# Offset rows and edge biases of a two-layer graph network: where they are added, and when shared one-hots are turned

## The chip, the core and the metric

The kernel is one program on one core of a Trainium2 chip. The metric is the device time of an execution in microseconds (us). The kernel before has a median of 10060.64 us over three runs (10058.67 to 10062.71). One further execution was recorded with the hardware profiler. It took 10882.62 us, and the durations in this document come from it.

## The reference, cut to what matters

A graph of 10,000 nodes (rows of 512 fp32 values) and 160,000 edges, sorted by `dst`, with eight attributes an edge, goes through two layers.

```python
# layer 0: a gated mixture of 4 experts, the top 2 of each node, each expert two SAGE convolutions
aggr = segment_sum(h[src], dst) * inv_deg
h = relu(aggr @ W_l + b_l + h @ W_r)              # twice for each expert
x = layernorm(x + sum(sel * top_v))
# layer 1: attention over the edges, 8 heads of 64, and a feed-forward net
z = layernorm(x)
q = (z @ Wq.T + bq).reshape(n, 8, 64)             # k and v in the same way
s = einsum('ehd,ehd->eh', q[src], k[dst]) / 8 + edge_attr_8
p = exp(s - segment_max(s, src)[src])
alpha = p / segment_sum(p, src)[src]
att = segment_sum(alpha[:, :, None] * v[dst], src) @ Wo.T + bo
x1 = x + att
ff = silu(layernorm(x1) @ W1.T + b1) @ W2.T + b2
out = layernorm(x + x1 + ff)
```

Two kinds of addends matter here. The *offsets* are rows of 512 that are the same for every node: `b_l` of each expert's second convolution, `bq`, `bk`, `bv`, `bo`, `b2`. The *edges' biases* are the eight values of `edge_attr_8` that are added to an edge's eight scores before the softmax.

## The kernel before, in words

Nodes are worked on in 79 blocks of 128 (`NB`). A block has four windows of 32 nodes (`NQ`, `W`), and a window has up to five chunks of 128 edges (`CAP`). Edges are brought to their nodes by gathers of whole rows (indirect DMAs that GpSimd issues) and by products of TensorE with one-hot matrices. There are three stages.

**First stage** (0 to about 3976 us of the trace). The first convolution of all experts (L1187) and the products of its result with the second convolution's neighbour weights (L1197), which go to memory as `y_tab`; the hidden rows themselves go to `h_tab`. They take the nodes' sums by one-hot products (L1148) of gathered rows; the one-hots are made on VectorE (L899, used by both stages). Beside this the edges are sorted for the attention (L1057). PE, VectorE, ScalarE and GpSimd run here in the order in which the program is written (`manual_schedule`). Near the end, in the third block group from the last, nine offset vectors go through `split_rows` (L715 to L730). A bf16 value holds fewer digits than an fp32 one, so the function cuts each offset into three rows of bf16 whose sum is the offset. It takes ten VectorE instructions on a tile of three partitions, eleven where a second vector is added first (`fold_s`, what the normalization's own offset contributes to queries, keys and values), and a load and a store on the SP queue. The rows are kept in memory as `rows_s`. From 3976 to about 4258 us the stage runs out.

**Second stage** (4258 to about 7720 us): the second convolution, its weighted sum over experts, two normalizations, and queries, keys and values. Only PE and GpSimd keep the written order; the scheduler places the work of VectorE, ScalarE and the SP queue. `bias_rows` (L732) loads seven offsets' three rows into a tile of 128 partitions that is zero elsewhere, and makes a tile of ones (`onesb`); a matmul of the two adds an offset to all rows of a product that stands in PSUM. In each block TensorE does, in this order:

1. Rounds 0 to 2 (L1417): one-hot products of the gathered `y` rows, accumulated in two PSUM tiles `p_ag`, 24 matmuls. Behind each round GpSimd issues four gathers (L1323) into buffers of a ring of 12.
2. Of the block before, the transposes of `z` (L1331), copied by ScalarE to `z_t`.
3. `own(b, 0)` and `own(b, 1)`: for an expert, a load of `hb` (L1375, six buffers, SP queue), four matmuls (L1378), the offset's matmul (L1379), and two VectorE products of the PSUM tile with the gate factors in `pick` (L1382 or L1385), which build the sums `t[0]` and `t[1]`. `own` of a block adds to tiles that `p_ag` joins at the block's end.
4. `fetch(b + 2)`: one-hots (L899) and gather addresses `ix` for the block after next.
5. Rounds 3 and 4 of L1417, the two-round burst.
6. `own(b, 2)` and `own(b, 3)`.
7. Of the block before, keys, values and queries: four matmuls each (L1340) and the offset's matmul (L1342). ScalarE copies keys (L1344) and values (L1346) into `kvt`, which goes to `kv_all` in memory; the query is scaled and cut into three bf16 parts by ScalarE and VectorE in turn (L1354 to L1359).
8. VectorE and ScalarE join `p_ag` and `t` (L1439), rectify (L1441), add to `x` (L1442) and normalize twice, to `x1` and `z`.

A row of `kv_all` has 1032 words (`KVW`): 512 of keys, and for each head 64 values and a one. The one makes the weighted sum yield the softmax's denominator as a 65th column.

**Third stage, the attention** (7720 to about 10880 us). A loop over windows (L1805), four steps `j` = 0 to 3 a block, with PE, VectorE, ScalarE and GpSimd in written order. A window's edges that sort to its own nodes fill four chunks; a fifth, shared by the block's four windows (`kvo`), takes the overflow. A step holds several windows at once, each at another point of its path:

- gathers of the rows of `kv_all` two steps ahead (L1543, through `pull` and `pull_over`);
- `expand` (L1780): one-hot products that bring the queries to the edges, in PSUM (`qe`); `expand_over` does it for the shared chunk;
- `score` (L1817): VectorE multiplies the keys by `qe`, in place, in two halves of two chunks; the reduction L1853 sums 64 products a head, and L1856 adds the edges' biases, which lie in `meta`. For the shared chunk `score_over` (L1794 to L1798) does the three things once a block, at j=3, and L1811 copies its scores to each window's `s`;
- `weigh`: a maximum over chunks into `wide` (L1682), its transpose on TensorE (L1684, "the row"), a maximum (L1687), a spread by matmul (L1689), subtraction (L1691), exponential (L1694, ScalarE), the product of one-hots and exponentials (L1703, three chunks on GpSimd, two on VectorE), weighted sums (L1717), denominators (L1722, L1723), scaling (L1726), a transpose (L1728);
- `turned` (L1565 to L1570): transposes of bf16 one-hots on TensorE and a copy by ScalarE; `turn_hots` for a window two steps ahead, and `over_t`, the four shared chunks of the next block, at the end of step j=2 (L1849). The PSUM tile `turns` holds the transposed `wide`, the spread maximum and these transposes;
- `open_block` (from L1510), behind j=1: one-hots of the block after next by comparison (L1518) and a copy (L1524).

Between these fixed places a small planner, `advance` (L1742), runs *jobs*: `front` (output weights, first residual, normalization, transposes), `back` (feed-forward, L1625 and L1635 with the Silu L1627 between them) for two blocks at once, `tail`. A job is a generator. It yields the cost of its next piece, and `advance(rate)` lets pieces run as long as credit lasts; a piece that yields 0 runs at most once at each call, so each `yield 0` puts what follows one call later. In `front` two of them stand between the offset's matmul (L1587) and `x2` (L1591), which VectorE adds; L1598, on GpSimd, adds the residual once more.

## Time and profile before

| | us |
|---|---|
| median of three runs | 10060.64 |
| the profiled execution | 10882.62 |
| its span, first to last instruction | 10880.8 |
| TensorE busy | 9845.5 |
| weight loads busy (beside TensorE) | 5639.8 |
| GpSimd busy | 6889.5 |
| VectorE busy | 5280.1 |
| ScalarE busy | 3011.4 |
| stretch of the first stage and its end | 0 to 4258 |
| stretch of the second stage | 4258 to 7720 |
| stretch of the attention | 7720 to 10880 |

The profiled execution is the longer one, by 8%; its mean granted clock of TensorE is 0.967. A group of the profile is one line with one engine and one form of operands: after the name and the shapes stand the count, behind the first bar the busy time in us and the mean duration of one instruction in ns, behind the second bar the idle time of the engine just ahead of these instructions, with what ended it. "issue" there is idle time for which the trace shows no wait. PE is TensorE, PEld its weight loads, DVE VectorE, ACT ScalarE, POOL GpSimd, SP the queue engine. GpSimd counts the time of its gathers' issue as busy (L1323 in the second stage, L1543 in the attention). The times of instructions are counted from the span's start.

### The profile page before, as it was taken

How to read it: one execution, taken by the hardware profiler on the slowest of the kernel's cores; microseconds unless marked ns; L12 is line 12 of the kernel's file. 1: busy time of each engine (PE TensorE's matmuls, PEld its weight loads, DVE VectorE, ACT ScalarE, POOL GpSimd, SP SyncE). 2: the span in 40 equal slices, each digit the busy share in tenths (PEclk: the TensorE clock that was granted, in tenths of full speed). 3: DMA queues.
4: the chain of work that ended last, by engine and by line, in shares of the span. 5: the costliest groups of instructions: out<-in, count | busy, mean ns of one | idle time of the engine just before them, and what ended most of it. 6: DMA issues, size and time to landing. Idle time of an engine off the chain costs nothing.

```text
span 10880.8 us, 168764 instructions
## 1 busy us (share of the span) xinstructions
PE 9845.5 (90%) x63574; PEld 5639.8 (52%) x63887; DVE 5280.1 (49%) x8244; ACT 3011.4 (28%) x5827; POOL 6889.5 (63%) x6736
## 2 busy tenths in 40 slices
PE   7999999999999988899998989899788888888888
PEld 4666666666666654333333333333455555555555
DVE  7888960000000021333333333333588888888886
ACT  1111111111111111111111111111266666666665
POOL 5566666666666664666666666666566666666664
PEclk9999999999999999999999999999799999999999
DMA  6544544444444434777777777777577777777774
GB/s 208 175 155 159 159 151 148 139 147 139 148 151 144 152 121 162 250 258 253 252 262 249 251 251 262 251 252 255 193 247 248 248 246 246 242 250 242 248 246 133
DMA packets 1076313, 2256.12 MB, mean 207 GB/s; under 512 B 250459, under 2 KB 500214, under 8 KB 1074720
## 3 DMA queue, kind: packets, MB, share of 16 engines
q0 software_dynamic: 588224, 1654.56, 47.8%
q1 hardware_dynamic: 479546, 576.99, 15.8%
q10 hardware_dynamic: 7718, 13.65, 0.4%
q8 instruction: 508, 8.32, 0.3%
q14 instruction: 317, 2.60, 0.1%
HBM read 2174.00 MB, written 378.96 MB: 235 GB/s over the span
## 4 chain that ended last, share of the span: by engine, by line
PE 78%; issue 8%; DVE 8%; ACT 4%; another core or an unknown queue 2%; DMA 1%; POOL 0%; ACTq 0%; SPq 0%; DVEq 0%; POOLq 0%
PE mm L1187 19%; PE mm L1378 10%; PE mm L1197 10%; PE mm L1340 8%; PE p_ag L1417 7%; PE p_ag L1148 4%; PE bank L1625 4%; PE bank L1635 4%; PE sums L1717 3%; DVE m L927 2%; PE bank L1585 2%; PE qe L1780 2%; DVE s L1853 2%; ACT L1627 1%
## 5 line engine op out<-in xcount | busy, mean ns | idle before, releaser
L1123 POOL DMA_INDIRECT ring<-in_x_dram,idx_t x1580 | 1929.2, 1221 | 1234.9 <-PE p_ag L1148 688.7
L1187 PE MATMUL mm<-tt,big 128*128 128x256 f32 (+1 forms) x8960 | 1980.9, 379 | 24.0 <-issue 23.4
L1187 PEld LDWEIGHTS mm<-tt,big 128*128 128x128 f32 x8960 | 1686.3, 191 | 324.8 <-issue 92.7
L1057 POOL DMA_INDIRECT sorted<-pay,addr x1250 | 1265.6, 1012 | 380.4 <-issue 356.5
L1378 PE MATMUL mm<-big,hb 128*128 128x512 f32 x2528 | 1241.9, 623 | 144.2 <-issue 127.8
L1323 POOL DMA_INDIRECT y<-y_tab,ix x920 | 932.8, 1014 | 479.7 <-issue 226.8
L1197 PE MATMUL mm<-wn,h 128*128 128x512 f32 x2528 | 1133.2, 598 | 18.6 <-issue 16.8
L1543 POOL DMA_INDIRECT kv<-kv_all,meta x948 | 974.0, 1027 | 260.1 <-issue 203.2
L1323 POOL DMA_INDIRECT ring<-y_tab,ix x660 | 686.5, 1040 | 558.5 <-PE p_ag L1417 272.5
L1189 ACT ACTIVATE h<-mm,bl 128x256 f32<-128x256 f32 (+1 forms) x640 | 294.8, 470 | 2527.3 <-PE mm L1187 1366.0
L1340 PE MATMUL mm<-big,z_t 128*128 128x512 f32 x1896 | 908.2, 619 | 60.6 <-DVE t L1385 28.9
L899 DVE TENSOR_TENSOR oh<-loc_t,iota_w 128x640 f32<-128x640 bf16 x158 | 129.9, 823 | 1687.7 <-remote 853.2
L1703 POOL TENSOR_TENSOR ohp<-oh,p 128x768 f32<-128x768 bf16 x316 | 466.1, 1475 | 695.5 <-ACT p L1694 694.9
L1378 PEld LDWEIGHTS mm<-big,hb 128*128 128x128 f32 x2528 | 486.1, 198 | 787.0 <-issue 741.3
L1197 PEld LDWEIGHTS mm<-wn,h 128*128 128x128 f32 x2528 | 468.3, 190 | 630.9 <-issue 617.3
L1441 ACT ACTIVATE t<-t,gsel 128x512 f32<-128x512 f32 x158 | 109.2, 722 | 2285.6 <-DVE t L1439 1644.9
L1625 PE MATMUL bank<-big,big 128*128 128x256 f32 (+1 forms) x2560 | 626.0, 388 | 91.8 <-ACT big L1627 66.7
L1417 PE MATMUL p_ag<-y,oh 128*32 128x512 f32 x3680 | 592.2, 600 | 76.6 <-issue 66.0
L1340 PEld LDWEIGHTS mm<-big,z_t 128*128 128x128 f32 x1896 | 371.1, 198 | 546.0 <-issue 481.6
L1635 PE MATMUL bank<-big,big 128*128 128x512 f32 x1264 | 592.3, 599 | 3.2 <-ACT big L1609 0.7
L1817 DVE TENSOR_TENSOR kv<-qe,kv 128x1024 f32<-128x1024 f32 x474 | 575.1, 1213 | 28.5 <-DMA kv<-kv_all,meta 28.4
L1625 PEld LDWEIGHTS bank<-big,big 128*128 128x128 f32 x2560 | 477.2, 195 | 210.0 <-ACT big L1627 103.7
(298 smaller groups left out, 14314.6 us busy)
## 6 DMA issues: line engine op xcount, KB each, us to landing
y_tab<-y SPq DMA_DIRECT2D x632, 256.0 KB
hb<-h_tab SPq DMA_DIRECT2D x316, 256.0 KB
h_tab<-h SPq DMA_DIRECT2D x156, 512.0 KB
kv_all<-kvt SPq DMA_DIRECT2D x79, 516.0 KB
xb<-in_x_dram SPq DMA_DIRECT2D x156, 256.0 KB
q_all<-q SPq DMA_DIRECT2D x79, 384.0 KB
q<-q_all SPq DMA_DIRECT2D x237, 128.0 KB
ring<-in_x_dram,idx_t POOLq DMA_INDIRECT x1580
```

The lines of the kernel that those rows point to most:

```text
L1057: inst = nc.gpsimd.indirect_dma_start(out=sorted1[:], out_offset=bass.IndirectOffsetOnAxis(ap=addr_i[:, c0 + c:c0 + c + 1], axis=0), in_=p ...
L1123: nc.gpsimd.indirect_dma_start(out=gbuf[i % GB], out_offset=None, in_=x, in_offset=bass.IndirectOffsetOnAxis(ap=window(idx_t, b)[:, j, c:c ...
L1187: nc.tensor.matmul(ph[:, :n], w[:, k, f * P:(f + 1) * P], tt[:, i, k, :n], start=(i + k == 0), stop=(i == 1 and k == KD - 1))
L1197: nc.tensor.matmul(py, h[:, k, i * P:(i + 1) * P], wn[e][:, k, :], start=(k == 0), stop=(k == KD - 1))
L1323: nc.gpsimd.indirect_dma_start(out=ybuf[i % YB], out_offset=None, in_=y_flat, in_offset=bass.IndirectOffsetOnAxis(ap=ahead[b][1][:, j, c:c ...
L1340: nc.tensor.matmul(po, z_t[:, k, :], wqkv[i][:, k, :], start=(k == 0), stop=False)
L1378: nc.tensor.matmul(pr, hb[:, k, :], wr[e][:, k, :], start=(k == 0), stop=False)
L1417: nc.tensor.matmul(p_ag[v][j * W:(j + 1) * W, :], oh[:, j * CAP + c, :], g[:, v * D:(v + 1) * D], start=(c == 0), stop=(c == CAP - 1))
L1543: nc.gpsimd.indirect_dma_start(out=to, out_offset=None, in_=kv_all[:], in_offset=bass.IndirectOffsetOnAxis(ap=blocks[b][0].bitcast(I32)[:, ...
L1625: nc.tensor.matmul(ph, up(f, k), z_t[:, k, :m], start=(k == 0), stop=(k == KD - 1))
L1635: nc.tensor.matmul(po, hid[:, k, i * P:(i + 1) * P], w2[k // KD][:, k % KD, :], start=(k == 0), stop=False)
L1817: nc.vector.tensor_tensor(k, qe.pop((w, g)), k, op=ALU.mult)
```

## The change

In the second stage the seven offset matmuls (L1379, L1342) go. The offsets come as rows of 512 fp32 on all 128 partitions, by seven broadcast loads on ScalarE's DMA queue at the stage's start, and VectorE adds them as it reads the product from PSUM. In `own` the sum goes to a new tile `mine`, from which the two products with `pick` then read. Keys and values go from PSUM through the addition straight into `kvt`, so ScalarE's two copies go; the query goes through `left`, which both the scaled copy and the subtraction then read. `hb` has four buffers instead of six. At the end of the first stage only `bo` and `b2` are split; for queries, keys and values the vector and its `fold_s` are added on one partition and stored (`bias_s`).

In the attention, keys get a 65th slot a head as values have it, so a row has 1040 words. ScalarE writes the edges' biases into the keys' slots: once at the head of each step for the four own chunks, and once a block, at the head of j=3 (for block 0, ahead of the loop), for the shared chunk. Products leave the slots out, and the reductions take 65 elements instead of 64, so L1856 and L1798 go. The turning of the shared one-hots moves from the end of step j=2 to its head. In `front` a `yield 0` is put at the start and one behind the offset's matmul.

The diff, cut to its core:

```diff
@@ -617,7 +617,9 @@
 VH = DH + 1
-KVW = D + H * VH
+
+HV = H * VH
+KVW = 2 * HV
@@ -688,7 +690,8 @@
     fold_s = dram.tile([3, D], F32, name="fold_s")
-    rows_s = dram.tile([3, NE + 5, D], BF16, name="rows_s")
+    bias_s = dram.tile([3, D], F32, name="bias_s")
+    rows_s = dram.tile([3, 2, D], BF16, name="rows_s")
     sorted1 = dram.tile([P * NC, WP], F32, name="sorted1")
@@ -712,12 +715,9 @@
-    def split_rows(full, mine, part, i, v, add):
+    def split_rows(full, mine, part, i, v):
         nc.sync.dma_start(full, bass.AP(tensor=v.tensor, offset=v.offset, ap=[[0, 3], [1, D]]))
-        if add is not None:
-            nc.sync.dma_start(mine, add.partition_broadcast(3))
-            nc.vector.tensor_add(full, full, mine)
         nc.vector.tensor_copy(part, full)
@@ -751,6 +751,9 @@
         return t
+
+    def by_head(t):
+        return t.rearrange("p (h d) -> p h d", h=H)[:, :, :DH]
@@ -1221,11 +1224,6 @@
-        vectors = [(a["L0_gnn_bl"][e, 1], None) for e in range(NE)] \
-            + [(a[f"L1_gnn_b{n}"], fold_s[i]) for i, n in enumerate("qkv")] \
-            + [(a["L1_gnn_bo"], None), (a["L1_gnn_b2"], None)]
-        vectors = [(i, *v) for i, v in enumerate(vectors)]
-
         with tc.manual_schedule(engines={ET.PE, ET.DVE, ET.Activation, ET.Pool}):
@@ -1275,15 +1273,24 @@
                     t1 = kp.tile([P, SC], BF16, name="pair")[:3]
-                    for v in vectors:
-                        split_rows(t3[:, :D], t3[:, D:2 * D], t1[:, :D], *v)
+                    for i, n in enumerate("qkv"):
+                        nc.sync.dma_start(t3[:1, :D], a[f"L1_gnn_b{n}"][None, :])
+                        nc.sync.dma_start(t3[:1, D:2 * D], fold_s[i:i + 1, :])
+                        nc.vector.tensor_add(t3[:1, :D], t3[:1, :D], t3[:1, D:2 * D])
+                        nc.sync.dma_start(bias_s[i:i + 1, :], t3[:1, :D])
+                    for i, n in enumerate(("bo", "b2")):
+                        split_rows(t3[:, :D], t3[:, D:2 * D], t1[:, :D], i, a[f"L1_gnn_{n}"])
...
         wr, wqkv = big[:4], big[4:7]
-        bias, onesb = bias_rows(wp, 0, NE + 3)
+        bias = wp.tile([P, NE + 3, D], F32, name="bias")
+        for e in range(NE):
+            nc.scalar.dma_start(bias[:, e, :], rows_bcast(a["L0_gnn_bl"][e, 1], D))
+        for i in range(3):
+            nc.scalar.dma_start(bias[:, NE + i, :], bias_s[i].partition_broadcast(P))
         gp = p2.enter_context(tc.tile_pool(name="p2g", bufs=1))
@@ -1338,21 +1345,21 @@
                     nc.tensor.matmul(po, z_t[:, k, :], wqkv[i][:, k, :], start=(k == 0),
-                                     stop=False)
-                nc.tensor.matmul(po, onesb, bias[:, NE + i, :], start=False, stop=True)
+                                     stop=(k == KD - 1))
+                row = bias[:, NE + i, :]
                 if i == 1:
-                    nc.scalar.copy(kv[:, :D], po)
+                    nc.vector.tensor_add(by_head(kv[:, :HV]), by_head(po), by_head(row))
                 elif i == 2:
-                    nc.scalar.copy(kv[:, D:].rearrange("p (h d) -> p h d", h=H)[:, :, :DH],
-                                   po.rearrange("p (h d) -> p h d", h=H))
+                    nc.vector.tensor_add(by_head(kv[:, HV:]), by_head(po), by_head(row))
                     nc.sync.dma_start(kv_all[r, :], kv)
...
                     s = DH ** -0.5
-                    nc.scalar.activation(q3[:, 0, :], po, AF.Copy, scale=s)
-                    nc.vector.scalar_tensor_tensor(left, po, s, q3[:, 0, :],
+                    nc.vector.tensor_add(left, po, row)
+                    nc.scalar.activation(q3[:, 0, :], left, AF.Copy, scale=s)
+                    nc.vector.scalar_tensor_tensor(left, left, s, q3[:, 0, :],
                                                    op0=ALU.mult, op1=ALU.subtract)
@@ -1371,18 +1378,20 @@
                 t = ts[b]
-                hb = dp.tile([P, KD, P], F32, name="hb", bufs=6)
+                hb = dp.tile([P, KD, P], F32, name="hb", bufs=4)
                 nc.sync.dma_start(hb, h_tab[s, :, e, :, i * P:(i + 1) * P])
...
                 for k in range(KD):
-                    nc.tensor.matmul(pr, hb[:, k, :], wr[e][:, k, :], start=(k == 0), stop=False)
-                nc.tensor.matmul(pr, onesb, bias[:, e, :], start=False, stop=True)
+                    nc.tensor.matmul(pr, hb[:, k, :], wr[e][:, k, :], start=(k == 0),
+                                     stop=(k == KD - 1))
+                mine = dp.tile([P, D], F32, name="mine")
+                nc.vector.tensor_add(mine, pr, bias[:, e, :])
                 for v in range(2):
                     if e == 0:
-                        nc.vector.tensor_scalar(t[v], pr, pick[:, v, b, e:e + 1], None,
+                        nc.vector.tensor_scalar(t[v], mine, pick[:, v, b, e:e + 1], None,
                                                 op0=ALU.mult)
                     else:
-                        nc.vector.scalar_tensor_tensor(t[v], pr, pick[:, v, b, e:e + 1], t[v],
+                        nc.vector.scalar_tensor_tensor(t[v], mine, pick[:, v, b, e:e + 1], t[v],
                                                        op0=ALU.mult, op1=ALU.add)
@@ -1475,7 +1484,7 @@
                                         op0=ALU.mult)
-        bias, onesb = bias_rows(wp, NE + 3, 2)
+        bias, onesb = bias_rows(wp, 0, 2)
         identb = wp.tile([P, P], BF16, name="identb")
@@ -1578,6 +1587,7 @@
             x1, att_t = rest.pop(b)
+            yield 0
             bank = yield from take()
@@ -1585,6 +1595,7 @@
             nc.tensor.matmul(po, onesb, bias[:, 0, :], start=False, stop=True)
+            yield 0
             yield 0
@@ -1713,7 +1724,7 @@
                     for h in range(4):
-                        v = D + (f * 4 + h) * VH
+                        v = HV + (f * 4 + h) * VH
                         nc.tensor.matmul(acc[h * W:(h + 1) * W, f, :], ohp[:, c, f * 4 + h, :],
@@ -1790,14 +1801,21 @@
                 if b < NB:
-                    k = kvo[b % 3][:, :D]
-                    nc.vector.tensor_tensor(k, qe.pop(b)[:, 0, :], k, op=ALU.mult)
+                    k = kvo[b % 3][:, :HV]
+                    nc.vector.tensor_tensor(by_head(k), by_head(qe.pop(b)[:, 0, :]), by_head(k),
+                                            op=ALU.mult)
                     s = s_over[b] = dp.tile([P, H], F32, name="s_over")
...
                                             axis=AX.X, op=ALU.add)
-                    nc.vector.tensor_add(s, s, blocks[b][0][:, SBC - 1, 2:])
+
+            def bias_over(b):
+
+                if b < NB:
+                    nc.scalar.copy(kvo[b % 3][:, :HV].rearrange("p (h d) -> p h d", h=H)[:, :, DH],
+                                   blocks[b][0][:, SBC - 1, 2:])
             expand_over(0)
+            bias_over(0)
             score_over(0)
@@ -1809,12 +1827,22 @@
                     nc.scalar.copy(s[:, SC_W, :], s_over[b])
+                    nc.scalar.copy(
+                        kv[:, :, :HV].rearrange("p c (h d) -> p c h d", h=H)[:, :, :, DH],
+                        blocks[b][0][:, j * SC_W:(j + 1) * SC_W, 2:])
+                if last:
+                    bias_over(b + 1)
+                if j == 2 and b + 1 < NB:
+                    over_t[b + 1] = turned(b + 1, range(SC_W, BC, CAP), "over_t", 2)
...
                         cs = GROUPS[g]
-                        k = kv[:, cs[0]:cs[-1] + 1, :D]
-                        nc.vector.tensor_tensor(k, qe.pop((w, g)), k, op=ALU.mult)
+                        k = kv[:, cs[0]:cs[-1] + 1, :HV].rearrange("p c (h d) -> p c h d", h=H)
+                        k = k[:, :, :, :DH]
+                        nc.vector.tensor_tensor(
+                            k, qe.pop((w, g)).rearrange("p c (h d) -> p c h d", h=H), k,
+                            op=ALU.mult)
@@ -1846,15 +1874,11 @@
                 advance(LATE)
-                if j == 2 and b + 1 < NB:
-                    over_t[b + 1] = turned(b + 1, range(SC_W, BC, CAP), "over_t", 2)
                 first = iter(())
...
                     nc.vector.tensor_reduce(s[:, :SC_W, :],
-                                            kv[:, :, :D].rearrange("p c (h d) -> p c h d", h=H),
+                                            kv[:, :, :HV].rearrange("p c (h d) -> p c h d", h=H),
                                             axis=AX.X, op=ALU.add)
-                    nc.vector.tensor_add(s[:, :SC_W, :], s[:, :SC_W, :],
-                                         blocks[b][0][:, j * SC_W:(j + 1) * SC_W, 2:])
                     first = weigh(w, s)
```

## The prediction

> **What bounds the kernel now.** I read first the busy times by stage, with stretches that I set at the stages' borders (us; busy time of TensorE, weight loads, VectorE, ScalarE, GpSimd; granted clock; DMA share; GB/s):
>
> ```profile
> 0.00:3976.00 3976.00, 3799.07 (x16507) 2516.39 (x16508) 1457.69 (x1473) 587.26 (x1141) 2547.68 (x2309) 0.99 0.49 155
> 3976.00:4258.00 282.00, 234.18 (x915) 156.69 (x914) 82.16 (x243) 36.24 (x72) 121.38 (x130) 0.90 0.34 112
> 4258.00:7720.00 3462.00, 3124.15 (x11651) 1201.59 (x11808) 1169.55 (x2166) 502.73 (x870) 2216.48 (x2243) 0.96 0.76 250
> 7720.00:10880.00 3160.00, 2688.14 (x34506) 1765.18 (x34660) 2570.65 (x4362) 1885.18 (x3744) 2003.96 (x2054) 0.96 0.74 236
> ```
>
> The first line is the first stage, the second its end (with the split of the offset vectors), the third the second stage, the fourth the attention. TensorE leads everywhere; in the attention VectorE stands close to it.
>
> For the second stage I then read its chain of work, cut at 240 characters, and its PE groups:
>
> ```profile
> by line: PE mm L1378 32.2%; PE mm L1340 24.2%; PE p_ag L1417 22.8%; issue 9.5%; another core or an unknown queue 4.4%; PE mm L1342 1.4%; PE pt L1331 1.3%; PE mm L1379 1.1%; DVE t L1385 0.8%; PE pt L1308 0.5%; DMA ring<-y_tab,ix 0.2%; DVE oh
> L1342 PE MATMUL mm<-rows,onesb 128*128 128x512 bf16 x235 | 89.1, 379 | 0.0
> PE p_ag L1417 <- issue: 96.8, 127, 1.6
> ```
>
> The chain is TensorE's queue. The two offset matmuls hold 2.5% of it. In the instruction list a block (43.2 us) falls into two parts. Part A runs from the three-round burst of L1417 to the end of the two-round burst. That second burst takes 3.64 us at best but 6.65 in the mean, and over 4.0 in 56 of 78 blocks: there TensorE waits for gathers. Part B (own 2 and 3, then keys, values, queries) waits for nothing. Its first microseconds run at half clock, as this 2 us stretch just behind such a wait shows:
>
> ```profile
> 5042.00:5044.00 2.00, 2.00 (x3) 0.84 (x3) 0.00 (x0) 0.00 (x0) 1.03 (x1) 0.50 0.00 0
> ```
>
> For the attention I read the groups (busy us, mean ns, idle before and its releasers) and one step in order of time:
>
> ```profile
> L1856 DVE TENSOR_TENSOR s<-s,meta 128x32 f32<-128x32 f32 x316 | 238.7, 755 | 10.9
> L1684 PE MATMUL turns<-ident,wide 128*128 128x128 f32 x316 | 95.5, 302 | 138.2 <-DVE den L1722 76.0 <-issue 33.3 <-ACT over_t L1570 22.2
> L1625 PE MATMUL bank<-big,big 128*128 128x256 f32 (+1 forms) x2560 | 626.0, 388 | 91.8 <-ACT big L1627 66.7 <-issue 16.0 <-ACT big L1609 0.4
> 8524.37 1.28 POOL L1598 TENSOR_TENSOR x<-x,x 128x512 f32<-128x512 f32 x1
> 8524.93 2.20 DVE L1856 TENSOR_TENSOR s<-s,meta 128x32 f32<-128x32 f32 x1
> 8525.58 1.49 POOL L1703 TENSOR_TENSOR ohp<-oh,p 128x768 f32<-128x768 bf16 x1
> 8527.65 0.69 DVE L1518 TENSOR_TENSOR oh<-meta,iota_q 128x512 bf16<-128x512 f32 x1
> ```
>
> The addition of the edges' biases (L1856) needs 0.19 us and holds VectorE for 0.755 in the mean. All of its 119 stretched instances overlap a GpSimd TENSOR_TENSOR and end as that ends. By step of a block they average 0.21 (j=0), 2.02 (j=1), 0.60 (j=2), 0.19 us (j=3).
>
> **What the Trainium skill says.** "SBUF — State Buffer", § Who interferes with whom: a VectorE instruction with two SBUF inputs contends with a GpSimd instruction that reads SBUF, one with a single SBUF input does not. The trace agrees: L1856 is stretched, the reduction L1853 beside the same GpSimd work keeps 2.27 us. It holds the other way too: an indirect DMA issue takes 0.99 us, but 1.29 in the mean of 62 beside L1358 and 1.58 beside L899. "TensorE: Matmul & The Clock Gate", § What's actually happening: after an idle window the array clock halves, and about 3.4 us of sustained work restore it; the 0.50 above agrees. The same page, § Wait — 56ns, not 53.3ns?, puts warm back-to-back matmuls of 512 columns at 215.7 ns; the chain has 0.22 us for L1342. "VectorE: DVE Perf Modes", § Mode 2×_2P: an fp32 tensor_scalar from SBUF can do two elements per cycle, through both ports; no long one stands in this trace.
>
> **The change, part by part**, in us of the profiled execution (10882.6).
>
> *End of the first stage.* Nine vectors are split on VectorE from 3977.1 to 4055.5, 78 us, between work in program order; one takes 7.0 (4042.98 to 4049.93). After: two splits (14) and three sums of a fetch of about 1.6, an addition of 0.68 and a store of about 2 (13), so 27: 50 us less. TensorE is idle 28 us in 3996 to 4077 while VectorE's L899 and gate additions stand behind the splits, and its clock is low until 4104. I take 25 of gain (5 to 40). Seven broadcasts (1.8 MB, at 250 GB/s 7 us) now stand beside the first gathers of the second stage: 4 of loss (0 to 7).
>
> *Second stage, TensorE.* 79 blocks lose 7 offset matmuls of 0.216 us: 1.51 us a block, 119 in all. Five lie in part B and count in full, 1.08. Two lie in part A; where gathers end it (56 of 78) they only lengthen the wait, so 0.43 x 0.28 = 0.12.
>
> *Second stage, VectorE.* Seven additions of 0.69 (L1355's kind, PSUM and SBUF) are new, 4.8 us beside 14.8 busy of 43.2. PSUM is freed earlier: one reader of 0.69 instead of two of 0.745. What could reach the path is the chain from p_ag to z: in the block at 5018 z stands at 5019.04 and TensorE takes it at 5022.72, 3.7 us of slack. One `mine` and the keys' addition come ahead of it (1.4), TensorE comes 0.65 earlier, so 1.6 remain: cost nothing; each microsecond beyond would be 79. Behind a waiting addition stand only VectorE's own next steps of that chain; GpSimd's gathers wait for it only through `ix`, two blocks ahead. ScalarE loses two copies of 0.57. With four `hb` buffers the loads wait for the same expert's matmuls one block before, still some 40 us ahead of use; in SP's new order kv_all, x1 and q_all follow loads that have long been released: nothing.
>
> *Ports.* The products with `pick` now read two SBUF operands (six) or may use both ports (two): eight new holders a block, in pairs. At L1358's +0.3 us a pair costs GpSimd 0.3 to 0.6; in part A only own 0's pair comes before the last gather that is needed, and that gather also waits for busy DMA queues: 0.1 a block (0 to 1.2). Stage: 1.08 + 0.12 - 0.1 = 1.1, x 79 = 87 (bounds -60 to 119).
>
> *Attention, VectorE.* L1856 (3.0 us a block) and L1798 (0.17) go; the reductions grow by 32 of 2048 elements (0.035 each). The strided products keep their 1024 elements, 1.21: taken as equal, at worst 0.1 more each. But VectorE's lateness reaches TensorE only at L1684, 138.2/79 = 1.75 us a block. In step j=1 TensorE comes later than the row (gap 0.07), and L1518, again with two SBUF inputs, would inherit the hold: nothing. For steps j=3 and j=0 (gaps 0.74 and 0.28) I take 0.25 from the 0.2 saved in each.
>
> *Attention, the turned one-hots.* At j=2's end L1684 waits 0.66 for the copy to over_t, behind four transposes of 0.055. Both go to the head of the step: 0.88 earlier there, 0.22 paid at the head. From the shared query products to the next row VectorE's serial path loses L1798 and L1856 but gains x2's addition: 5.27 before, about 5.5 after, 0.25 lost. Net 0.41. VectorE's wait ahead of L1591 (131 us) mostly turns into one ahead of the shared scores.
>
> *Attention, ScalarE.* A copy of 32 elements a step and one of 8 a block are new (L1811's kind, 0.20): 1.05 us a block, at the head, where it waits for all four gathers. Behind it stand the Silu that L1625 waits for (1.16 us a block now) and Exp; in j=2 also over_t's 0.58. I take 0.2 (0 to 1.2). Stage: 0.25 + 0.41 - 0.2 = 0.46, x 79 = 36 (bounds -50 to 138). Rows of 1040 instead of 1032 words add 0.8% to gathers that the products waited 28 us for: nothing.
>
> Sum: 25 - 4 + 87 + 36 = 144 of 10882.6, 1.32%. The median of the runs is 10060.64, 0.924 of the profiled one; I carry the ratio over: 10060.64 x (1 - 0.0132) = 9927.
>
> **Rivals.** (1) *VectorE is the attention's real pace*: all 138 us before L1684 go instead of 36, so 246 in all, 9833. For it: VectorE is busy 2571 of 3160 and the chain visits it every step. Against: 85% TensorE, whose largest gap (L1717, 184 us) has no releaser. (2) *Gathers are the second stage's pace and ScalarE eats the attention's gain*: only 21 remain, 10041. For it: 56 of 78 late bursts. Against: part B waits for nothing. (3) *Slower, by the port*: the eight holders delay the descriptors. All four in part A at 0.3 make the second burst 1.2 us later, and the longer wait costs one more 3.4 us at half clock, 1.7: 2.9 against 1.2 gained, +134 in the stage, 57 gained elsewhere, so +77: 10132. It turns the sign from an added wait of 1.8 us a block on (144/79, gains included). For it: L899's 1.58. Against: only one pair falls ahead of the last gather.
>
> **How the numbers follow.** The forecast has 0.50 (own range 9860 to 9990), rival 1 0.22, rival 2 0.17, rival 3 0.11. 0.2%, 20 us, is about what a measurement of this kernel can tell from no change. Rival 2 lies on that line, half of it faster. Faster 0.80, same 0.09, slower 0.11. The range 9810 to 10055 leaves out rival 3 and the far tail of rival 1.
>
> **What would show it.** Right: no PE matmul of 128x512 bf16 in the second stage, its stretch some 85 us shorter; the second burst as late as before; no gap at L1684 for over_t; the VectorE hold seen again at the one-hots' comparison in j=1; L1625's idle a little up. Wrong: indirect issues of 1.3 us and more in number, a second burst over 7.5 us, VectorE waiting for nothing while TensorE waits at the row.

## The result, and the profile after

The kernel after takes 10026.2 us, the kernel before 10062.71 (medians of 7 runs each): ratio 0.9965, 95% interval 0.9953 to 0.9976. The change makes the kernel 36 us faster, where 133 were forecast (9927 against 10060.64): the time lies inside the stated range, near its upper end of 10055, and the gain is about a quarter of the forecast. The first recording of the kernel before, on which the prediction rests, ran 8% longer than every timed run; a second one (*before_again*, 10057.12 us) agrees with them, so the comparison below uses it.

Stretches of the second recording of the kernel before (us of the stretch; busy time of TensorE, weight loads, VectorE, ScalarE, GpSimd; granted clock; DMA share; GB/s):

```profile
0.00:3999.30 3999.30, 3893.34 (x17420) 2645.18 (x17421) 1541.93 (x1716) 629.62 (x1213) 2642.49 (x2439) 0.99 0.51 162
3999.30:6986.50 2987.20, 2907.38 (x11611) 1154.45 (x11767) 1169.39 (x2161) 517.28 (x868) 2215.35 (x2243) 1.00 0.85 289
6986.50:10055.30 3068.80, 2615.56 (x34546) 1717.43 (x34700) 2575.38 (x4367) 1863.43 (x3746) 2016.33 (x2054) 0.97 0.76 243
```

The same of the kernel after:

```profile
0.00:3978.80 3978.80, 3892.40 (x17420) 2649.69 (x17421) 1501.86 (x1644) 629.49 (x1213) 2644.70 (x2439) 0.99 0.52 163
3978.80:6934.60 2955.80, 2834.17 (x11216) 1103.09 (x11214) 1487.19 (x2714) 429.07 (x710) 2243.47 (x2243) 0.99 0.85 293
6934.60:10025.00 3090.40, 2648.41 (x34700) 1736.13 (x34700) 2446.29 (x3973) 1868.94 (x4103) 2045.00 (x2054) 0.96 0.76 243
```

The first stage gained 20.5 us and the second 31.4, and the attention lost 21.6. VectorE is busy 129 us less in the attention, as meant, and the stage is longer all the same. Where it went shows in the chains of work. Second stage, before_again:

```profile
by line: PE mm L1378 36.5%; PE mm L1340 19.1%; PE p_ag L1417 18.5%; DMA y<-y_tab,ix 9.2%; DMA ring<-y_tab,ix 5.9%; issue 3.4%; POOL y L1323 1.5%; PE pt L1331 1.5%; POOL ring L1323 1.3%; PE mm L1342 1.2%; PE mm L1379 1.1%; PE pt L1308 0.6%; 
```

Second stage, after:

```profile
by line: issue 18.9%; PE mm L1385 18.3%; DMA y<-y_tab,ix 17.2%; DMA ring<-y_tab,ix 10.5%; PE p_ag L1426 10.2%; PE mm L1347 6.6%; POOL y L1330 6.3%; POOL ring L1330 4.6%; POOL sorted L1060 3.0%; PE pt L1338 1.3%; DMA sorted<-pay,addr 1.2%; P
```

Gathers have gone from 15% of that chain to 28%, GpSimd's own steps from 3% to 14%, and "issue", here nearly all idle time just ahead of GpSimd's issues, from 3.4% to 18.9%. Attention, before_again:

```profile
by line: PE bank L1625 10.6%; PE bank L1635 10.5%; DVE s L1853 10.0%; PE bank L1585 8.9%; ACT L1694 6.1%; DVE s L1856 4.6%; issue 4.3%; DMA kv<-kv_all,meta 4.2%; ACT L1627 3.3%; PE qe L1780 3.3%; PE sums L1717 2.7%; DVE kv L1817 2.6%; ACT b
```

Attention, after:

```profile
by line: DMA kv<-kv_all,meta 22.5%; issue 9.1%; PE bank L1646 8.0%; DVE s L1879 7.8%; PE bank L1636 7.0%; ACT L1638 4.7%; ACT L1705 4.5%; PE bank L1595 3.1%; ACT big L1638 2.5%; PE sums L1728 2.1%; ACT L1678 2.0%; PE qe L1791 1.8%; ACT oh_t
```

L1856 has left it, with 4.6%; the gathers of keys and values have grown from 4.2% to 22.5%. In both stages the change took work off the path that the prediction read, and gathers took its place.

### The profile page after: what moved, and what is told of

Read it like the earlier page. It is cut to its first block, busy times and chain, and to the rows that moved or that the text cites. A ratio compares the mean times of both kernels' runs of the same rounds, so it can differ in the third digit from the quotient of the medians.

```text
span 10025.0 us, 168607 instructions
## 1 busy us (share of the span) xinstructions
PE 9375.0 (94%) x63334; PEld 5488.9 (55%) x63334; DVE 5435.3 (54%) x8330; ACT 2927.5 (29%) x6026; POOL 6933.2 (69%) x6736
## 4 chain that ended last, share of the span: by engine, by line
PE 55%; DMA 16%; issue 9%; DVE 8%; ACT 7%; POOL 5%; POOLq 0%; ACTq 0%; DVEq 0%; SPq 0%
PE mm L1190 21%; PE mm L1200 10%; DMA kv<-kv_all,meta 7%; PE mm L1385 5%; DMA y<-y_tab,ix 5%; PE p_ag L1151 3%; DMA ring<-y_tab,ix 3%; PE p_ag L1426 3%; PE bank L1646 2%; DVE s L1879 2%; DVE m L930 2%; PE bank L1636 2%; PE mm L1347 2%; POOL y L1330 2%; ACT L1638 1%
## 5 line engine op out<-in xcount | busy, mean ns | idle before, releaser
L1126 POOL DMA_INDIRECT ring<-in_x_dram,idx_t x1580 | 1897.1, 1201 | 1014.3 <-PE p_ag L1151 570.3
L1385 PE MATMUL mm<-big,hb 128*128 128x512 f32 x2528 | 1120.4, 597 | 1.7 <-DMA hb<-h_tab 1.7
L1347 PE MATMUL mm<-big,z_t 128*128 128x512 f32 x1896 | 829.6, 594 | 0.7 <-ACT z_t L1340 0.7
L1388 DVE TENSOR_TENSOR mine<-mm,bias 128x512 f32<-128x512 f32 x316 | 218.5, 692 | 1065.2 <-PE mm L1385 1063.6
L1636 PE MATMUL bank<-big,big 128*128 128x256 f32 (+1 forms) x2560 | 671.7, 410 | 89.6 <-ACT big L1638 89.5
L1636 PEld LDWEIGHTS bank<-big,big 128*128 128x128 f32 x2560 | 501.2, 204 | 207.9 <-ACT big L1638 113.4
```

The costliest lines, as they stand in the source:

```text
L1126: nc.gpsimd.indirect_dma_start(out=gbuf[i % GB], out_offset=None, in_=x, in_offset=bass.IndirectOffsetOnAxis(ap=window(idx_t, b)[:, j, c:c ...
L1347: nc.tensor.matmul(po, z_t[:, k, :], wqkv[i][:, k, :], start=(k == 0), stop=(k == KD - 1))
L1385: nc.tensor.matmul(pr, hb[:, k, :], wr[e][:, k, :], start=(k == 0), stop=(k == KD - 1))
L1636: nc.tensor.matmul(ph, up(f, k), z_t[:, k, :m], start=(k == 0), stop=(k == KD - 1))
```

## The experiments

| run | ratio to before | interval | first stage / second / attention, us |
|---|---|---|---|
| before_again | one run | | 3999 / 2987 / 3069 |
| after | 0.9965 | 0.9953 to 0.9976 | 3979 / 2956 / 3090 |
| stage2_rows | 0.9944 | 0.9930 to 0.9957 | 3979 / 2950 / 3077 |
| attention_all | 1.0023 | 1.0016 to 1.0031 | 3998 / 3001 / 3088 |
| slots_alone | 1.0021 | 1.0014 to 1.0027 | 3998 / 2986 / 3093 |
| slots_late | 1.0031 | 1.0019 to 1.0044 | 3999 / 2984 / 3092 |
| slots_by_vector | 1.0036 | 1.0023 to 1.0050 | 3999 / 2989 / 3105 |
| slots_compare_moved | 1.0016 | 1.0008 to 1.0024 | 4002 / 3003 / 3102 |
| slots_late_over | 0.9982 | 0.9975 to 0.9988 | 3999 / 2978 / 3048 |
| over_alone | 0.9949 | 0.9935 to 0.9962 | 4000 / 2998 / 3020 |
| rows_and_over | 0.9899 | 0.9884 to 0.9914 | 3979 / 2962 / 3018 |
| rows_over_late | 0.9897 | 0.9882 to 0.9912 | 3979 / 2962 / 3023 |
| after_no_yields | 0.9931 | 0.9917 to 0.9945 | 3979 / 2946 / 3060 |
| after_late_over | 0.9931 | 0.9917 to 0.9944 | 3982 / 2964 / 3069 |
| after_both | 0.9896 | 0.9880 to 0.9911 | 3979 / 2953 / 3025 |
| half_before | one run | | 4002 / 3009 / 3072 |
| half_after | one run | | 3982 / 3038 / 2974 |
| sorting_out_before | one run | | 4001 / 2867 / not compared |
| sorting_out_rows | one run | | 3979 / 2805 / not compared |

The stage lengths are those of one recording each. Kernels with the same second stage differ there by 12 us (2987 and 2998, 2950 and 2962), so the lengths are read for large differences alone. In the diffs below `...` stands for lines left out.

### The change in two halves

> The kernel before, unchanged, recorded a second time: its first recording took 10882.6 us against a median of 10060.6, and its first stage, which the change doesn't touch, took 4258 us there against 3979 in the kernel after. Both theories expect a span near 10,060 and a first stage near 4,005 us (25 more than after, for the split). Theory 1 (gathers are the second stage's pace, so the matmuls that went bought little): second stage within 40 us of the 2956 us that it takes in the kernel after. Theory 2 (the second stage gained as predicted, 90 us, and the attention gave it back): second stage near 3045, attention near 3010, under the 3090 of the kernel after.

> The kernel before with the second stage's part alone: offsets added by VectorE as rows, two splits instead of nine, four hb buffers; rows of 1032 words and the attention as before. Theory 1 (gathers are the pace): -20 to -45 us, of which about 25 at the end of the first stage; the second stage's TensorE waits for gathers where the matmuls were. Theory 2 (the attention gave the gain back): -100 to -120 us.

> The kernel before with the attention's part alone: biases in the keys' 65th slot, shared one-hots turned at the head, two more yields in the planner's front; the second stage with its offset matmuls. Theory 1: -10 to +15 us, or as predicted -36. Theory 2: +60 to +80 us.

The edits are the diff of the change, cut at the border of the second stage and the attention. The halves multiply to 0.9944 x 1.0023 = 0.9967, the change's 0.9965: nothing shows that they act on each other. Stage2_rows gained 56 us, more than theory 1 expected and half of what theory 2 did; the attention lost 23, less than theory 2 wants. So both halves fall short, each in its own stage.

### What paces the second stage

TensorE's waits there (us in total, times, longest), before_again:

```profile
PE p_ag L1417 <- DMA y<-y_tab,ix: 45.6, 50, 2.8
PE p_ag L1417 <- DMA ring<-y_tab,ix: 24.3, 29, 3.5
```

and after:

```profile
PE p_ag L1426 <- DMA y<-y_tab,ix: 77.1, 69, 3.1
PE p_ag L1426 <- DMA ring<-y_tab,ix: 39.6, 40, 3.5
```

In the list of instructions most of it (52 of 70 us before, 98 of 117 after) lies in one place: round 2 of the three-round burst, just behind part B. A round needs 1.92 us; round 2 takes 3.62 before and 4.71 after. So 1.09 of the 1.51 us of matmuls that left a block came back there. Only some 0.6 of it is recorded as waiting; the rest hides in busy time. The matmuls of a block's four windows start within 0.02 us of each other when all four gathers have landed, and apart when they haven't: round 2 starts in 6.2 batches in before_again and in 7.1 after, where 4.1 do when no gather is late (sorting_out_before, below). A stretch of GpSimd's queue of the kernel after shows why (start, duration, idle before):

```profile
5022.43 1.10 POOL L1060 DMA_INDIRECT sorted<-pay,addr  x1 [0.31 <-DMA y<-y_tab,ix]
5023.84 1.01 POOL L1060 DMA_INDIRECT sorted<-pay,addr  x1 [0.31 <-issue]
...
5027.95 1.04 POOL L1330 DMA_INDIRECT ring<-y_tab,ix  x1 [0.30 <-issue]
5029.30 1.01 POOL L1330 DMA_INDIRECT ring<-y_tab,ix  x1 [0.30 <-issue]
```

GpSimd issues without a pause: 20 gathers and 7.04 sorting DMAs a block, each with 0.30 us in front that the profile counts as idle. Busy time (2218 us / 79 = 28.1) plus 27 x 0.30 makes 36.2 of a block of 36.8 us. GpSimd at "2243 of 2956" is full. In before_again the same sum is 35.9 of 37.3 us.

> The kernel before with gathers of half the bytes in the second stage and the attention (same number of gathers, same indices; it leaves out the second half of each gathered row, so the neighbours' second half and the attention's values are not computed). The second stage of the kernel before takes 2987 us, 80 of them TensorE idle. If the bytes of the gathers are its pace, it falls to about 2900 here, close to TensorE's busy time. If GpSimd's issue or VectorE is the pace, it stays within 20 us of 2987. Attention: a fall by 30 to 80 us if the landing of the gathers is in its way.

> The kernel after with the same halved gathers (same parts left out). Second stage, against half_before: if bytes are the pace there, the seven matmuls a block are worth their full 100 to 119 us now, instead of the 31 that the whole gathers leave; if not, again 30 to 40. Attention, against half_before: if the late gathers keep VectorE's gain from showing, the kernel after is now 10 to 60 us shorter there instead of 21 longer; if something else than gathers makes it longer, it stays 15 to 30 longer.

```diff
-                    out=ybuf[i % YB], out_offset=None, in_=y_flat,
+                    out=ybuf[i % YB][:, :D], out_offset=None, in_=y_half,
...
-                out=to, out_offset=None, in_=kv_all[:],
+                out=to[:, :KVW // 2], out_offset=None,
+                in_=kv_all.rearrange("n (two v) -> (n two) v", two=2),
```

For the second stage this missed: it got longer, not shorter. Round 2 did fall (2.46 and 3.50 us), and TensorE's waits for gathers with it (70 to 20 us in half_before, 117 to 52 in half_after), so bytes matter to how long a gather takes to land. But in half_before VectorE waits for the sorting's own loads in 32 places (341 us in all, 97 in before_again), and TensorE behind VectorE in 14 (91 us). Why those loads are late with half the traffic is open. That bytes aren't the whole pace is clear from half_after: round 2 still waits.

> The kernel before, with the seven sorting DMAs that GpSimd issues between the gathers of each block of the second stage put behind the stage (all 556 in one row there, so the whole kernel gets some 600 us longer; only the stage's blocks are read). A block holds 20 gathers and 7.04 sorting DMAs at 0.99 + 0.30 us: 35.1 us, with three small copies about 36 of GpSimd, against 37.2 measured. If GpSimd's issue is the pace, its floor falls to 26 us and a block takes what TensorE needs, 17.0 + 18.2 = 35.2 us. If TensorE and the bytes are the pace, a block stays at 36.8 to 37.3.

> Stage2_rows with the same move. If GpSimd's issue was the pace, the seven matmuls are now worth their full 1.5 us a block: 33.7 us against sorting_out_before's 35.2, so 119 us in the stage's blocks where the whole change had 31 to 37. If the bytes or VectorE's additions are the pace, the difference stays near 0.5 us a block.

```diff
                 rounds(range(3))
-                drive(scat, 4)
...
                 rounds(range(3, CAP))
-                drive(scat, 3)
```

The second stage of sorting_out_before, then of sorting_out_rows:

```profile
4001.00:6868.20 2867.20, 2841.10 (x11769) 1147.78 (x11767) 1163.13 (x2127) 518.65 (x868) 1647.87 (x1628) 0.99 0.85 299
```

```profile
3978.80:6784.20 2805.40, 2766.39 (x11216) 1111.35 (x11214) 1483.57 (x2678) 429.15 (x710) 1683.14 (x1628) 1.00 0.88 306
```

The 556 DMAs, in one row behind the stage, make the whole kernels 10626 and 10541 us long. With them out of GpSimd's queue the stage before is 120 us shorter, at more GB/s (299 for 289), and round 2 waits for nothing (1.90 us): the length of that queue was in the stage's way, beside the time to landing that the halved gathers shortened. The sorting's loads, its small copies and 7 of the stage's 864 MB left the stage as well; no run tells them apart from the issues. The matmuls are now worth 62 us (0.82 a block, 35.62 against 34.80) instead of 31 to 37, but not 119: rounds 3 and 4, whose gathers are issued in the same block, take 2.33 and 2.60 us in sorting_out_rows against 1.94 and 2.10 in sorting_out_before. Behind the first wait stood a second one. The additions are paid too: GpSimd's DMA issues in the second stage take 2218 us after against 2194 before, 0.3 us a block, on a queue that is full.

### What lost in the attention

> The attention's biases in the keys' 65th slot alone; shared one-hots turned at the end of j=2 as before, and no further yields. The prediction's steps give 20 us gained on VectorE and 16 lost on ScalarE: -4 us. If VectorE is the attention's pace: -100 and more. If ScalarE's copies at the head of a step delay the Silu and Exp behind them: +20 to +80.

> The kernel before with the shared one-hots turned at the head of j=2 alone: no slots, no further yields. The prediction's steps: no wait for over_t at the row of j=2 (0.66 us a block) and at most 0.47 paid elsewhere, -15 to -32 us. If what comes next is late anyway (the gathers of j=3): -5 to +8.

```diff
+                if j == 2 and b + 1 < NB:
+                    over_t[b + 1] = turned(b + 1, range(SC_W, BC, CAP), "over_t", 2)
...
                 advance(LATE)
-                if j == 2 and b + 1 < NB:
-                    over_t[b + 1] = turned(b + 1, range(SC_W, BC, CAP), "over_t", 2)
```

The slots lose 22 us, which lies where the expectation had put a delay by ScalarE's copies, and the turn gains 51, more than expected; together with the yields they lose 23. Groups of before_again in the attention (mean ns, and idle before, are the last two numbers ahead of a releaser):

```profile
L1856 DVE TENSOR_TENSOR s<-s,meta 128x32 f32<-128x32 f32 x316 | 241.5, 764 | 10.9
L1518 DVE TENSOR_TENSOR oh<-meta,iota_q 128x512 bf16<-128x512 f32 x79 | 62.5, 792 | 0.0
L1708 POOL TENSOR_TENSOR over<-over,far 128x40 f32<-128x40 f32 x316 | 85.2, 270 | 0.0
L1817 DVE TENSOR_TENSOR kv<-qe,kv 128x1024 f32<-128x1024 f32 x474 | 575.1, 1213 | 71.2 <-DMA kv<-kv_all,meta 70.3
```

and of the kernel after:

```profile
L1527 DVE TENSOR_TENSOR oh<-meta,iota_q 128x512 bf16<-128x512 f32 x79 | 169.0, 2139 | 0.0
L1719 POOL TENSOR_TENSOR over<-over,far 128x40 f32<-128x40 f32 x316 | 119.1, 377 | 0.0
L1843 DVE TENSOR_TENSOR kv<-qe,kv 128x1024 f32<-128x1024 f32 x474 | 576.4, 1216 | 256.2 <-DMA kv<-kv_all,meta 255.1
L1681 DVE RECIPROCAL rs<-rs 128x1 f32<-128x1 f32 x158 | 24.7, 156 | 101.2 <-ACT rs L1678 101.2
```

The hold has passed from L1856 to the one-hots' comparison (792 to 2139 ns), as predicted. But it reaches GpSimd too: the small addition to `over` (L1719) grows, all of it at j=0, from 0.28 to 0.71 us, and VectorE waits 185 us more for gathers. One step of the kernel after in order of time, VectorE and GpSimd alone:

```profile
8522.53 2.32 DVE L1527 TENSOR_TENSOR oh<-meta,iota_q 128x512 bf16<-128x512 f32 x1
8522.80 1.50 POOL L1714 TENSOR_TENSOR ohp<-oh,p 128x768 f32<-128x768 bf16 x1
8524.23 0.74 POOL L1719 TENSOR_TENSOR over<-over,far 128x40 f32<-128x40 f32 x1
...
8525.13 1.02 POOL L1552 DMA_INDIRECT kv<-kv_all,meta  x1 [0.16 <-issue]
```

The comparison is stretched by GpSimd's product, and then makes the addition wait until it ends. Behind the addition stand the four gathers of the window of j=3. Averaged over the blocks (the first three and the last are left out), in us from the maximum (`wide`) of j=0:

| kernel | product on GpSimd ends, j=0 | gathers of j=3 begin | their issue ends | second scores of j=3 end | `wide` j=1 | `wide` j=3 | `wide` of the next j=0 |
|---|---|---|---|---|---|---|---|
| before_again | 10.18 | 10.57 | 15.52 | 24.63 | 10.21 | 30.16 | 37.50 |
| over_alone | 10.17 | 10.59 | 15.55 | 24.14 | 10.17 | 29.50 | 36.86 |
| slots_alone | 9.98 | 10.81 | 15.94 | 25.07 | 7.89 | 29.95 | 37.87 |
| slots_by_vector | 10.14 | 10.96 | 16.07 | 24.97 | 8.77 | 30.56 | 37.94 |
| slots_late_over | 10.01 | 10.18 | 15.37 | 24.41 | 8.11 | 29.46 | 37.23 |
| after | 9.35 | 10.19 | 15.30 | 23.85 | 7.26 | 29.15 | 37.76 |
| after_late_over | 9.42 | 9.59 | 14.79 | 23.39 | 7.20 | 28.79 | 37.41 |
| after_no_yields | 10.15 | 10.98 | 16.10 | 24.66 | 8.09 | 29.57 | 37.36 |
| after_both | 10.02 | 10.20 | 15.40 | 24.14 | 8.03 | 29.13 | 36.97 |
| half_after | 9.37 | 10.20 | 15.34 | 20.95 | 6.87 | 28.24 | 36.19 |
| rows_and_over | 10.17 | 10.58 | 15.53 | 24.11 | 10.20 | 29.50 | 36.84 |
| rows_over_late | 10.08 | 10.26 | 15.41 | 23.99 | 10.21 | 29.53 | 36.87 |

With the slots alone step j=1 ends 2.3 us earlier, and 0.2 of it is left at j=3: there the scores wait for gathers that hang on GpSimd. With half the bytes the scores of the kernel after end 2.9 us earlier (23.85 to 20.95), and the attention of half_after is 98 us shorter than that of half_before (2974 against 3072; 10 to 60 were expected), where with whole rows the change made it 22 longer. In half_before the same bytes bought nothing (3072 against 3069): landing became the limit through the change.

> As slots_alone, but ScalarE writes the edges' biases behind the Exp of the window before (ahead of the next gathers' issue), no longer at the head of the step, so that nothing on ScalarE waits for four gathers. Slots_alone is 1.0021 of before. If the copy at the head, with Silu and Exp queued behind it, is what makes it slower: 0.996 to 1.000. If the gathers' lateness or the clock lost to a changed pattern of idle windows is the cause, whatever the copy's place: 1.001 to 1.003.

> As slots_alone, but VectorE writes the edges' biases into the keys' slots, just ahead of each reduction (a copy with one SBUF input), and ScalarE writes none. Slots_alone is 1.0021 of before. If ScalarE as a link between the gathers and the scores is what costs, this is 0.995 to 1.000 of before. If it is the rows of 1040 words, or VectorE's gain coming back as waits and half clock, 1.001 to 1.003.

```diff
-                    nc.scalar.copy(
+                    nc.vector.tensor_copy(
                         kv[:, :, :HV].rearrange("p c (h d) -> p c h d", h=H)[:, :, :, DH],
                         blocks[b][0][:, j * SC_W:(j + 1) * SC_W, 2:])
```

The diff is that of slots_by_vector, where the copy also moves from the head of the step to just ahead of the reduction; slots_late keeps `nc.scalar.copy` and moves it behind the third `next(one, 1)` of the step. Neither is better. Slots_by_vector has no such copy on ScalarE and loses as much, with the addition at j=0 at 0.69 us: the hold is there whichever engine copies. This doesn't clear ScalarE, since VectorE now pays for the copies (110 us for the own chunks, and `wide` j=1 comes 0.9 us later than in slots_alone). What ScalarE's copies cost shows from the maximum of j=3 to the next one of j=0: 7.34 us in before_again, 7.38 in slots_by_vector, 7.92 in slots_alone, and 7.8 in slots_late_over, after_no_yields and after_both, which have the copies too. ScalarE's copy waits for all four gathers, the Silu comes later, and TensorE waits for it. Here is one group of before_again (TensorE's feed-forward, L1625), then the copy and the same feed-forward (L1630) in slots_alone:

```profile
L1625 PE MATMUL bank<-big,big 128*128 128x256 f32 (+1 forms) x2560 | 638.1, 394 | 114.0 <-ACT big L1627 105.0 <-ACT big L1609 0.2
L1824 ACT COPY kv<-meta 128x32 f32<-128x32 f32 x237 | 59.4, 250 | 262.3 <-DMA kv<-kv_all,meta 227.2 <-issue 34.6
L1630 PE MATMUL bank<-big,big 128*128 128x256 f32 (+1 forms) x2560 | 664.3, 406 | 142.5 <-ACT big L1632 137.9 <-ACT big L1614 0.4 <-ACT oh L1529 0.2
```

In slots_alone 0.43 us a block of this wait lies in that stretch, in before_again and slots_by_vector none. Slots_late can't say: its additions take 0.29 us, but its reductions now wait for the copies, as this group of it shows:

```profile
L1874 DVE TENSOR_REDUCE s<-kv 128x32 f32<-128x2080 f32 x237 | 549.8, 2320 | 318.8 <-ACT kv L1856 318.8
```

> As slots_alone, with the one-hots' comparison (open_block) behind step j=2 instead of j=1, where no GpSimd product runs. If slots_alone is slower since the comparison inherits the hold and keeps GpSimd's addition to over at j=0 0.71 us instead of 0.28 ahead of the gathers of j=3: the addition takes 0.28 again, and the time is 0.997 to 1.000 of before. If the rows of 1040 words or the missing addition itself do it: 1.002 as slots_alone.

```diff
                 if j == 1:
-                    open_block(b + 2)
...
+                if j == 2:
+                    open_block(b + 2)
```

This missed, and in an instructive way. The addition at j=0 still takes 0.66 us, since the next operation of VectorE with two SBUF inputs, its own half of the one-hots' product, inherits the hold:

```profile
7794.60 1.49 POOL L1708 TENSOR_TENSOR ohp<-oh,p 128x768 f32<-128x768 bf16 x1
7795.19 1.46 DVE L1708 TENSOR_TENSOR ohp<-oh,p 128x512 f32<-128x512 bf16 x1
7796.04 0.73 POOL L1713 TENSOR_TENSOR over<-over,far 128x40 f32<-128x40 f32 x1
```

and the moved comparison holds the addition of j=1 (0.68). The Trainium skill's page "SBUF — State Buffer", § Who interferes with whom, says that issue order, not the kind of operation, decides who blocks; these lines agree. So the addition must be moved, not its neighbour:

> The kernel after, with GpSimd's addition to over (it follows the one-hots' product) issued behind the next gathers instead of ahead of them. If the path that sets the attention runs from the one-hots' product of j=0 on GpSimd through this addition and the gathers of j=3 to the scores of j=3, the 0.71 us that the addition takes there comes off: 35 to 56 us under the kernel after, 0.991 to 0.993 of before. If VectorE or ScalarE sets it: within 8 us of the kernel after.

> Slots_alone with GpSimd's addition to over behind the gathers. If the inherited hold of that addition (0.43 us a block, 34 us in all) is why slots cost 22 us, they now gain some 10: 0.998 to 1.000 of before. If the rows of 1040 words or something else costs: 1.001 to 1.002.

```diff
             weighted(nc.gpsimd, OWN, CAP)
-            nc.gpsimd.tensor_tensor(over, over, far, op=ALU.add)
             yield
+            nc.gpsimd.tensor_tensor(over, over, far, op=ALU.add)
             weighted(nc.vector, 0, OWN)
```

Both came as the theory of the GpSimd path has it. After_late_over takes 34 us off the kernel after, just under the 35 to 56 expected; slots_late_over turns the slots' loss of 22 us into a gain of 18. The gathers of j=3 begin 0.60 and 0.63 us earlier, and 0.36 and 0.49 of that reach `wide` of j=3. On rows_and_over the same edit does nothing:

> Rows_and_over with GpSimd's addition to over behind the gathers. On the same path it takes 0.28 us in each step: 10 to 22 us less than rows_and_over, 0.988 of before. If the path is another: no difference.

0.9897 against 0.9899, where 10 to 22 us were expected. Without slots the addition isn't held. The gathers of j=3 begin 0.3 us earlier (10.26 for 10.58) and the block is no shorter (36.87 for 36.84), so there they aren't what sets it.

> The kernel after without the two further yields in the planner's front. In the kernel after, the way from the row of j=3 to that of j=0 takes 8.5 us against 7.3 in over_alone, and VectorE waits 0.9 us a block there for the first residual's square root. If the yields put that there: 0.989 to 0.993 of before. If the slots do: 0.996 to 0.998, as the kernel after.

```diff
             x1, att_t = rest.pop(b)
-            yield 0
...
             nc.tensor.matmul(po, onesb, bias[:, 0, :], start=False, stop=True)
-            yield 0
             yield 0
             yield 0
```

The yields cost 34 us, at the edge of what was expected (0.9931 for 0.989 to 0.993). They moved the first residual's normalization into the way from j=3 to j=0, 8.61 us (37.76 - 29.15) with them and 7.79 without, where VectorE waits for ScalarE's square root (L1681 above, 101 us; 23 in before_again). In after_both that wait is down:

```profile
L1679 DVE RECIPROCAL rs<-rs 128x1 f32<-128x1 f32 x158 | 24.8, 157 | 29.1 <-ACT rs L1676 28.8
```

> The kernel after with both edits: no further yields in front, and GpSimd's addition to over behind the gathers. Each alone took 34 to 37 us off the kernel after. If they lie on different stretches of a block (j=3 to j=0, and j=0 to the gathers of j=3), they add up: 0.989 to 0.990 of before, as fast as rows_and_over. If both shorten the same wait: 0.992 to 0.993.

> Stage2_rows and over_alone together, without slots and without the further yields. They gained 0.56% and 0.51% alone, in different stages: 0.989 to 0.990 of before (about 9955 us) if the two are independent, which would beat both kernels.

The two edits add up: 0.9965 to 0.9896, 105 us under before. Rows_and_over, the second stage's half and the turn without slots and yields, gets the same, 0.9899. Both beat both kernels by more than 0.6%.

## Why the prediction was wrong

The sum had 144 us. By stages, 25 less 4 became 20.5, 87 became 31, and 36 gained became 22 lost.

*End of the first stage: right.* 20.5 us measured; the 25 for the splits and the 4 for the broadcasts aren't told apart.

*Second stage: failed at "Five lie in part B and count in full, 1.08".* Part B itself waits for nothing, as said, but what follows it does: of the 1.51 us removed, 1.09 reappear in round 2 (3.62 to 4.71 us). The prediction has no term for the length of GpSimd's queue. With the 0.30 us ahead of each issue it needs some 36 us a block: there was room in the 43.2 of the recording that the prediction had, and hardly any in the 37.3 of the second one. In the first the late gathers were seen in the two-round burst; in the second they stand in the three-round burst, behind part B. Rival 2 named the mechanism; it left the second stage too little (measured 31 to 37, not nearly nothing), and its 10041 is nearest to the measured 10026. The port term was mis-sized, 0.3 us a block for 0.1. The 1.58 us that the prediction quotes for an issue beside L899 was one issue; all that overlap L899 in that stage average 1.31.

*Attention, VectorE: failed at "L1518, again with two SBUF inputs, would inherit the hold: nothing".* That the hold is inherited was right. Priced at nothing, it costs 34 to 39 us, since the holder keeps GpSimd's addition that stands ahead of the next gathers. That the 20 us put down for the shorter way to the row agree with what the slots bring in slots_late_over (18) is luck: there the way from j=0 to j=3 is 0.70 us a block shorter (30.16 to 29.46), not 0.25, and the way from j=3 to j=0 is 0.43 longer.

*The turned one-hots: right alone, too small a price for the yields.* The wait for over_t at the row goes, and the turn alone brings 51 us where 0.88 - 0.22 = 0.66 a block, 52 us, were put down for it. The loss of 0.25 us a block (20 us) for x2's later addition should have been 34, and by another way: the normalization behind it moved into the stretch from j=3 to j=0.

*ScalarE: right in mechanism, too small.* 16 us were put down for copies that wait for four gathers with the Silu behind them. The wait for the Silu is there (105 to 138 us), and the way from j=3 to j=0 is 0.43 us a block longer in slots_late_over and 0.58 in slots_alone, 34 and 46 us; without the copies on ScalarE it is 0.04. Slots_by_vector isn't faster for it, as VectorE then pays.

In sum, as ratios of 10060: slots +22 (of them the hold 39, from 1.0021 - 0.9982), turn -51, yields +34 make +5; the measured half is +23. The rest, 18, is less than the intervals together leave open (about 25). The runs hint where it lies: with the slots in place the turn brings less, 34 us with the hold (0.9944 x 1.0021 = 0.9965 to after_no_yields' 0.9931) and 30 without it (0.9944 x 0.9982 = 0.9926 to after_both's 0.9896). VectorE waits 46 and 49 us for the copy of over_t there, 21.5 in over_alone; on ScalarE that copy now stands behind the new one. No run isolates this. Rival 3, slower by the port, had the right kind of cause in the wrong stage.

## What to carry to other kernels

Before a gain on one engine is counted, look up what its consumer also waits for, and when that was issued: here two stages were a step away from waiting for gathers, and a GpSimd queue of DMA issues was full at 76% busy. A hold on the shared port wasn't removed with the operation that showed it; it went to the next one with two SBUF inputs, and what counted was what stood behind it on GpSimd. A short copy on an engine with room still delays what is queued behind it, if the copy has to wait. When several edits are bundled, time each alone: here the turn had a gain of 0.5% inside, cancelled by the slots and by two yields that looked free.

## What the runs showed of the hardware

- An indirect DMA costs GpSimd 1.00 us of issue (median of the kernel after) and 0.30 us ahead of it, seen at 92% of the issues.
- A late gather costs TensorE more than the recorded wait: in round 2, 1.09 us a block more, of which 0.6 is idle and the rest matmuls of single windows that no longer start together (7.1 batches for 6.2, 4.1 with nothing late).
- The port holds in both directions within one pair: GpSimd's product stretched VectorE's comparison from 0.69 to 2.3 us, and the comparison then kept GpSimd's 40-element addition from 0.28 to 0.74 us.
- With gathers of half the bytes the data came earlier: the second scores of j=3 end 5.6 us behind the last issue instead of 8.6 (15.34 to 20.95, 15.30 to 23.85).
- `tensor_scalar` with its input in SBUF (`mine`) takes 0.515 us for 128x512 in the kernel after, 0.746 from PSUM in before_again (means of 158 each). The prediction says that no long one with its input in SBUF stands in its trace; eight do, 0.48 us each (L1476).
- Equal idle time doesn't mean equal time at half clock: slots_alone idles no longer than before_again on TensorE (451 and 453 us of the attention) but has 44 stretches at half clock instead of 30, 245 us instead of 198. This isn't why the slots lose: slots_late_over has 46 stretches and 245 us too, and its attention is 45 us shorter (3048 for 3093).
